# Queries of the first two units by seven products, and half of two weight sums moved to VectorE

## The chip, the cores and the metric

The kernel runs on one core of one Trainium2 chip. The core has five engines with a queue of instructions each: TensorE (PE in the profile; its weight loads are PEld), VectorE (DVE), ScalarE (ACT), GpSimd (POOL) and SyncE (SP, which here only issues DMAs). Each engine takes its instructions in order, and waits between engines are semaphores. The metric is the device time of one execution in microseconds (us), the median of several runs. All arrays are float32.

## The reference

One transformer layer with the normalisation behind each half. Its input is `x` of 2 batches x 512 tokens x 512 channels. Cut to what matters:

```python
q = x @ Wq + bq                 # 32 heads of 128
k = x @ Wk + bk; v = x @ Wv + bv   # 8 groups of 128
q, k = rope(q), rope(k)         # x1*cos - x2*sin, x1*sin + x2*cos
scores = q @ k.T / sqrt(128), causal mask, softmax
ctx = probs @ v                 # 4 query heads share one group's k and v
x = layernorm(x + ctx @ Wo + bo)
y = x @ W_base.T + b_base       # then 4 chosen experts of rank 8
alpha = softmax(log(prior[active] + 1e-12) + (x @ router_W.T + router_b)[active])
y += sum over experts e of 2 * alpha_e * (x @ lora_A[e].T) @ lora_B[e].T
out = layernorm(x + y)
```

Everything has to be computed; `active` (which experts) is an input, so the experts' rows are gathered on the chip.

## The kernel before

**Units and slots.** The work is cut into 16 units: unit `u` is one group of four query heads (`R = 4`) in one batch, with 512 queries and 512 keys (`S`). A unit has 16 slots, one for every block of 32 queries x 4 heads (`QB`, `BLK`). The function `slot(T)` writes out what each engine does in slot `T`, in order: the query products of a later unit, key and value products, output products of an earlier unit, `score(T)`, then, each some slots behind, the maximum with the mask (`masked_max`, DVE), the exponentials (ACT), the reciprocals and transposes (DVE), the trip of the probabilities through DRAM (`blocks_out` in slot 4p+7 and `blocks_in` in slot 4p+9 for tile p) and `weigh(p, j)` from slot 4p+12 (probabilities times v). Slots run from `T_BEGIN = -8`; score 0 is in slot 0. Work that fits no regular place is hung onto a slot with `put(slot, f)` and runs at that slot's end. The order is written by hand (`manual_schedule`), so each engine's queue is exactly the order in which `slot` and the code ahead of it call; only the first lines (constants, loads) are ordered by the framework.

**Before slot 0.** Lines 1034 to 1061 are a preamble: four transposes of x tiles of batch 0 into `xT` (channels on partitions), keys of unit 0 (`k_mm`, `k_rope`), `expert_rows` (thirteen small integer operations on DVE that make the gathers' indices from `active`, then two gathers on POOL's queue), the queries of unit 0, four tiles of v, and the transposes of batch 1. Queries of unit 0 are plain: for each head four matmuls of 128x128x512 into one PSUM bank (`q_mm`, `proj_mm`, L355). Queries of unit 1 are plain too, one such matmul in each of the slots -8 to 7.

**Seven products.** From unit 2 on, two heads at a time (`k` is 0 or 1, the pair) are computed as a 2x2 block product with seven block products in place of eight (Strassen-Winograd): `q_products(u, k, step)`, steps 1, 2, 6, 5, 7, 4, 3, each two matmuls of 128x128x256 (`product`, L434). It needs sums of the weights, `w_sums` (four operations on POOL, L421 to L424, the last of which writes over a block of the weight tile itself), sums of x, `x_sums` (four operations of 128x512 per batch on DVE, L413), and leaves partial results in two half banks, `qx` and `qy`:

- step 1 writes qx; ACT copies it out (`q_copy` "p1"). Step 6 adds onto qx after that copy; copy "u2". Step 7 adds onto qx after that; copy "u3". Step 4 adds onto qx after that; copy "c21". So each of 6, 7, 4 and the next pair's step 1 waits for one copy.
- step 2 writes qy; DVE adds it to what "p1" left (`q_sum` "p1"). Step 5 begins qy anew after that sum; `q_sum` "u3" reads it after copy "u3"; step 3 adds onto qy after that; `q_sum` "u2" reads it, and the next pair's step 2 waits for that sum.

In slot T the step is given by (T+24) mod 8: 2, 6, 5, 7, none, 4, 3, and the next pair's 1. The fifth of eight slots has no query product.

**The rotation** (`rope_step`) is three DVE operations per head (L368, L371, L375), then an addition on POOL (L376) into `qT` or `kT`. Plain queries are read from PSUM by these; queries of the seven products have been copied to SBUF before and are read there.

**Moved pieces.** `prior_weights` (the logarithm of the prior on ACT, small DVE operations, one tiny matmul `pl`), `gather_experts` (six gathers on POOL's queue), `lora_weights` (transposes of the gathered rows on PE into the bank `wx`, copied out by DVE, L285, L286 and L292) and the addition of the output bias to the eight x tiles (POOL, L885) hang on slots by `put`. Tiles of v for batch 1 and the next groups also go through the bank `wx`, in slots -1, 1, 3, 5, 11, 13, 15, 17.

**Output weights.** `ctx @ Wo` also goes by seven products; it needs four sums of Wo's blocks per weight set, `wo_sums` (L627): t1 = b12 - b11, t2 = b22 - t1, b12 = b22 - b12 in place, t4 = b21 - t2. For weight sets of two units they are on DVE; for the last two that need them (sets 6 and 7, of one unit each, `single`) all four are on POOL in the slot ahead of the unit's first output product. The third slot of the eight uses t2 (`wx<-wt,cs`).

Of the kernel before, what the change touches and what calls it, by code (L numbers as in the profile page):

```python
# [12 lines left out]
ALU = mybir.AluOpType  # L13
# [5 lines left out]
R = H // G  # L19
D = 128  # L20
# [9 lines left out]
def postln_layer_kernel(  # L30
# [59 lines left out]
    def unit(u):  # L90
        return units[u]

    def set_of(u):
        return u // B if u < MIXED else MIXED // B + u - MIXED

    def set_units(n):
        return [u for u in range(NU) if set_of(u) == n]
# [86 lines left out]
    for r in range(QB):  # L184
        nc.gpsimd.tensor_copy(maskw[ts(r, BLK), S - BLK :], tri[ts(r, BLK), r, :])
    nc.gpsimd.memset(eps_sb, LN_EPS)
    for z in zt:
        nc.gpsimd.memset(z, 0.0)

    bqk = setup.tile([NBIAS, D], F32, name="bqk")  # L190
    nc.scalar.dma_start(out=bqk[:H, :], in_=bq.rearrange("(h d) -> h d", d=D))
# [104 lines left out]
    def prior_weights(step):  # L296

        if step == 0:
            pr_eps = setup.tile([EA, 1], F32, name="pr_eps")
            nc.vector.tensor_scalar(pr_eps, pr_act, PRIOR_EPS, None, ALU.add)  # L300
            pr["lp"] = setup.tile([EA, 1], F32, name="lp")
            nc.scalar.activation(pr["lp"], pr_eps, AF.Ln)
        elif step == 1:
            lpb = setup.tile([EA, 1], F32, name="lpb")
            nc.vector.tensor_tensor(lpb, pr["lp"], rb_act, ALU.add)
            ones = setup.tile([EA, P], F32, name="ones")
            nc.vector.memset(ones, 1.0)
            pr["rep"] = setup.tile([EA, P], F32, name="lp_rep")
            nc.vector.tensor_scalar(pr["rep"], ones, lpb, None, ALU.mult)
        else:  # L310
            pl = ps_wo.tile([P, EA], F32, tag="wx", name="pl")
            nc.tensor.matmul(pl, lhsT=pr["rep"], rhs=ident[:EA, :EA], start=True, stop=True)
            nc.vector.tensor_copy(lp_bc, pl)
# [37 lines left out]
    def proj_mm(key, pool, tag, wt, cols, b, c):  # L351
        if c == 0:
            psq[key] = pool.tile([P, S], F32, tag=tag, name="pp")
            in_psum.add(key)
        nc.tensor.matmul(  # L355
            psq[key], lhsT=wt[:, c, cols], rhs=xT[:, c, ts(b, S)], start=(c == 0), stop=(c == KC - 1))
# [31 lines left out]
    def k_rope(u, part):  # L388
        if part == 0:
            k_of(u)  # L390
        rope_step(("k", u), H + unit(u)[0], part, kT[u])

    def q_mm(u, r, c, pool, tag):

        g, b = unit(u)
        proj_mm(("q", u, r), pool, tag, wqk["q", set_of(u), r // 2], ts(r % 2, D), b, c)

# [5 lines left out]
    ws = {}  # L406
    halves = {}

    def x_sums(b, step):
        b11, b12, b21, b22 = (  # L410
            xT[:, CH * k : CH * (k + 1), b * S + a * TH : b * S + (a + 1) * TH] for k in range(2) for a in range(2))
        t1, t2, t3, t4 = (xs[:, b, k] for k in range(4))
        nc.vector.tensor_tensor(  # L413
            *((t1, b12, b11), (t2, b22, t1), (t3, b22, b12), (t4, b21, t2))[step], ALU.subtract)

    def w_block(n, k, head, c_half):
# [115 lines left out]
    def q_rope(u, r, part):  # L532
        if u not in qT:
            qT[u] = work.tile([P, UNIT, R, BLK], F32, tag="qT", name=f"qT_{u}")
        rope_step(("q", u, r), unit(u)[0] * R + r, part, qT[u][:, :, r, :])
# [325 lines left out]
    def put(slot, f):  # L861
        extra.setdefault(slot, []).append(f)
# [4 lines left out]
        for c in range(KC):  # L867
            v_mm(gg, t, c, pool, tag)

    put(T_BEGIN, gather_experts)  # L870
    for n, gg, t in [(2 * t - 1, 0, TPB + t) for t in range(TPB)] + [(2 * t + 11, 1, t) for t in range(TPB)]:
        put(n, lambda gg=gg, t=t: v_tile(gg, t, ps_wo, "wx"))
        put(n + 1, lambda gg=gg, t=t: v_out(gg, t))
    for n in range(TPB):
        put(n, lambda n=n: x_sums(0, n))
        put(n + 12, lambda n=n: x_sums(1, n))
    for k in range(3):
        put(-4 + k, lambda k=k: prior_weights(k))
        if k < 2:
            put(12 + 4 * k, lambda k=k: lora_weights(k))  # L880
    put(1, lambda: load_q(1, 1))
    put(6, lambda: load_wv(1))
    put(17, lambda: load_wo(1))
    for t in range(NT):
        put(2 + t, lambda t=t: nc.gpsimd.tensor_tensor(x_sb[:, t, :], x_sb[:, t, :], bo_bc, ALU.add))  # L885

    def q_from(u, k):

# [33 lines left out]
    def wo_from(u):  # L922
        return UNIT * u + LAG_WO
# [3 lines left out]
    for n in range(NSETS - 2):  # L927
        single = len(set_units(n)) == 1
        for k in range(4):
            put(wo_from(set_units(n)[0]) + (-1 if single else (0, 1, 1, 3)[k]),  # L930
                lambda n=n, k=k, engine=nc.gpsimd if single else nc.vector: wo_sums(n, k, engine))


    weigh_at = {}
# [13 lines left out]
    def slot(T):  # L948

        uq, step = divmod(T + 24, UNIT)  # L950
        kq, step = divmod(step, 8)
        now = B <= uq < NU
        if now and step != 7 and step != 4:
            q_products(uq, kq, {0: 2, 1: 6, 2: 5, 3: 7, 5: 4, 6: 3}[step])
        un, kn = (uq, 1) if kq == 0 else (uq + 1, 0)
        if B <= un < NU and step == 7:
            q_products(un, kn, 1)
        plain_q = T - T_BEGIN < UNIT and divmod(T - T_BEGIN, QB)
        if plain_q:
            r, c = plain_q  # L960
            q_mm(1, r, c, *q_banks[r])
        uk, l = divmod(T + UNIT, UNIT)
        if 0 < uk < PLAIN_K and l < KC:
            k_mm(uk, l)
        kv, o = kv_at(T)
        if kv and o in KV_STEPS:
            kv_products(*kv, KV_STEPS[o])
        kw, sw = divmod(T - LAG_WO, 8)
        products = 0 <= kw < LAST // 8
        if products:  # L970
            wo_products(kw, sw)
        plain = plain_at.get(T)
        if plain:
            p, step_o = plain
            wo_mm(p, 2 * step_o)
            wo_mm(p, 2 * step_o + 1)
        if 0 <= T < T_END:
            score(T)
        for part, j in weigh_at.get(T, ()):
            weigh(part, j)  # L980

        if now and step in (0, 2, 4, 6):
            q_copy(uq, kq, ("p1", "u2", "u3", "c21")[step // 2])
        if kv and KV_OUT.get(o) in KV_ON_ACT:
            kv_out(*kv, KV_OUT[o])
        for part, j in weigh_at.get(T - 1, ()):
            if j == parts[part][1]:
                context_out(part)

        if 0 <= T - 3 < T_END:  # L990
            normalise(T - 3)
        if 0 <= T - 1 < T_END:
            masked_max(T - 1)
            exponentials(T - 1)
        if products:
            wo_adds(kw, sw)
        if sw == 0 and 0 < kw <= LAST // 8:
            wo_adds(kw - 1, 8)
        if now and step in (1, 5, 7):
            q_sum(uq, kq, {1: "p1", 5: "u3", 7: "u2"}[step])  # L1000
        if kv and o in KV_OUT and KV_OUT[o] not in KV_ON_ACT:
            kv_out(*kv, KV_OUT[o])
        if 0 <= T - 2 < T_END:
            reciprocals(T - 2)
        if 0 <= T - 4 < T_END:
            blocks_transposed(T - 4)
            if (T - 4) % QB == QB - 1:
                blocks_out((T - 4) // QB)
        if T % QB == 1 and 0 <= T // QB - 2 < NP:
            blocks_in(T // QB - 2)  # L1010
        if 0 <= (T - LAG_WO + 1) // 8 < LAST // 8 and (T - LAG_WO + 1) % 8 == 0:
            ctx_sums((T - LAG_WO + 1) // 8)

        ur, sr = divmod(T + 24 - 7, UNIT)
        kr, sr = divmod(sr, 8)
        if B <= ur < NU and sr < 6:
            q_rope(ur, 2 * kr + (sr < 3), sr % 3)
        r, part = divmod(T - T_BEGIN - QB, QB)
        if 0 <= r < R and part < 3:
            q_rope(1, r, part)  # L1020
        k_slots = (4, 5, 6) if uk < PLAIN_K else (11, 13, 14) if uk < NU - 1 else (3, 5, 6)
        if 0 < uk < NU and l in k_slots:
            k_rope(uk, k_slots.index(l))
        if plain and step_o:
            wo_out(p)
        for f in extra.pop(T, ()):
            f()
# [1 line left out]
    ctx.enter_context(tc.manual_schedule())  # L1029

    spare = ((ps_wo, "wx"), (ps_wo, "wy"), (ps_ctx, "ctx"), (ps_sc, "sc"))
    q_banks = ((ps_q, "qx"), (ps_q, "qy"), (ps_q, "qx"), (ps_wo, "wy"))

    idle = ps_sc.tile([P, 2 * P], F32, tag="sc", name="idle")
    for _ in range(3):
# [5 lines left out]
    nc.vector.tensor_copy(bqkT, tb)  # L1041
    for c in range(KC):
        k_mm(0, c)
    for part in range(3):
        k_rope(0, part)
    expert_rows()

    for r in range(R):
        for c in range(KC):
            q_mm(0, r, c, *q_banks[r])  # L1050
        for part in range(3):
            q_rope(0, r, part)
        if r == 2:
            for t in range(TPB, NT):
                transpose_token_tile(xT[:, :, ts(t, P)], x_sb[:, t, :], *spare[t % 2 + 2], nc.scalar.copy)
        elif r:
            v_tile(0, r // 2, *spare[r // 2 * 2])
            v_out(0, r // 2)
    for t in range(2, TPB):
        v_tile(0, t, *spare[t % 2 * 2])  # L1060
        v_out(0, t)

    T_SETUP = 20
    for T in range(T_BEGIN, T_SETUP):
# [189 lines left out]
```

## Time and profile before

| what | value |
|---|---|
| median of 5 runs | 825.78 us (825.49 to 826.32) |
| the profiled execution's own time | 825.63 us |
| its span, first to last instruction | 823.6 us |
| granted TensorE clock | 0.998 |
| busy: PE / DVE / ACT / POOL | 814.0 / 598.1 / 378.6 / 327.7 us |
| first key matmul of unit 0 | 7.75 us |
| slot -8 begins on PE (first query matmul of unit 1) | 34.1 us |
| slot 0 begins on PE | 43.3 us |
| slot 8 begins on PE | 62.0 us |
| slot 13 begins on PE | 71.5 us |

The table's last rows are starts of instructions in the timeline, counted from the span's start. The profile is of one execution. In the timeline a row has start, length, engine, source line, operation, output<-inputs, shape, and in brackets how long the engine was idle ahead of it and what ended that; rows of DVE and POOL overlap those of PE. "x4" joins four instructions: a float32 matmul stands as two instructions. In the chain of work that ended last, a row has start, length and what ran.

### The profile page before, as it was taken

To read this page: it belongs to the slowest core of one execution; us is meant where nothing else is said; L and a number is where in the kernel's file an instruction comes from. 1 tells how busy PE (TensorE), PEld (TensorE's weight loads), DVE (VectorE), ACT (ScalarE), POOL (GpSimd) and SP (SyncE) were. 2 spreads that over 40 slices of the span, in tenths; PEclk is the share of its full clock that TensorE was granted. 3 is DMA by queue.
4 is the path that set the end of the run, shared out by engine and by line. 5 is a ranking of instruction groups with operands and counts; after the bars stand their busy time and mean duration, and the time that the engine had idled before them with its cause. 6 is when DMAs were issued, how large, how long until landed. Compare 5 with 4: busy or idle time off the path is not lost.

```text
span 823.6 us, 11178 instructions
## 1 busy us (share of the span) xinstructions
PE 814.0 (99%) x3381; PEld 596.6 (72%) x3381; DVE 598.1 (73%) x1964; ACT 378.6 (46%) x1058; POOL 327.7 (40%) x374
## 2 busy tenths in 40 slices
PE   8999999999999999999999999999999999999997
PEld 5567777777777778777777878777777777555565
DVE  5368877677879886787867786787867678974445
ACT  1236454453545454545535454445535454563253
POOL 6464343511534445322443245353445625410032
PEclk9999999999999999999999999999999999999999
DMA  9015627445455636364544536365544636574211
GB/s 306 21 52 150 202 73 197 121 122 159 125 170 139 182 90 209 87 160 146 149 146 115 179 90 205 91 185 173 136 134 120 194 83 204 142 255 142 76 38 64
DMA packets 84414, 115.99 MB, mean 141 GB/s; under 512 B 6525, under 2 KB 64237, under 8 KB 82306
## 3 DMA queue, kind: packets, MB, share of 16 engines
q1 hardware_dynamic: 83682, 114.98, 48.4%
q8 instruction: 27, 0.44, 0.2%
q0 software_dynamic: 448, 0.14, 0.1%
q14 instruction: 33, 0.27, 0.1%
q10 hardware_dynamic: 224, 0.16, 0.1%
HBM read 71.21 MB, written 44.04 MB: 140 GB/s over the span
## 4 chain that ended last, share of the span: by engine, by line
PE 93%; DVE 3%; POOL 2%; ACT 1%; DMA 1%; issue 0%; SPq 0%; DVEq 0%; POOLq 0%
PE pc L602 16%; PE sc L546 14%; PE qx L434 11%; PE wx L434 11%; PE qy L434 9%; PE wy L434 8%; PE pp L355 5%; PE kx L434 4%; PE vx L512 4%; PE py L767 3%; PE po L674 3%; PE pv L338 3%; PE tp L275 1%; PE py L808 1%; DMA x_sb<-_attn_hidden_states_dram 1%
## 5 line engine op out<-in xcount | busy, mean ns | idle before, releaser
L554 DVE CUSTOM_DVE_ANT_0 sc<-sc,maskw 128x288 f32<-128x288 f32 (+15 forms) x256 | 114.2, 446 | 146.3 <-PE sc L546 144.7
L561 ACT ACTIVATE p<-sc,nmax 128x288 f32<-128x288 f32 (+15 forms) x256 | 124.1, 485 | 203.4 <-DVE nmax L554 180.6
L602 PE MATMUL pc<-pT,v 128*128 128x512 f32 x320 | 165.3, 599 | 0.0
L546 PE MATMUL sc<-kT,qT 128*128 128x160 f32 (+15 forms) x512 | 161.9, 398 | 0.2 <-ACT p L561 0.2
L376 POOL TENSOR_TENSOR qT<-q,t 128x512 f32<-128x512 f32 x56 | 76.4, 1364 | 171.4 <-DVE q L375 171.4
L569 ACT ACTIVATE p<-p,den 128x288 f32<-128x288 f32 (+15 forms) x256 | 133.2, 521 | 0.0
L546 PEld LDWEIGHTS sc<-kT,qT 128*128 128x128 f32 x512 | 95.9, 190 | 23.5 <-issue 9.6
L609 ACT ACTIVATE ctxT<-pc,bqkT 128x512 f32<-128x512 f32 x64 | 44.0, 687 | 117.6 <-PE pc L602 117.6
L421 POOL TENSOR_TENSOR cs<-ctxT 128x256 f32<-128x256 f32 x28 | 22.2, 793 | 157.8 <-PE wy L434 93.7
L577 DVE STREAM_TRANSPOSE zt<-p 128x128 f32<-128x128 f32 (+2 forms) x192 | 81.6, 425 | 0.0
L602 PEld LDWEIGHTS pc<-pT,v 128*128 128x128 f32 x320 | 57.1, 190 | 18.7 <-issue 5.7
L470 ACT COPY q<-qx 128x256 f32<-128x256 f32 x112 | 41.3, 369 | 36.5 <-PE qx L434 36.5
L434 PE MATMUL qx<-xs,wq 128*128 128x256 f32 x224 | 58.0, 381 | 0.0
L434 PE MATMUL wx<-wo,ctxT 128*128 128x256 f32 x224 | 57.6, 379 | 0.0
L434 PEld LDWEIGHTS qx<-xs,wq 128*128 128x128 f32 x224 | 41.4, 190 | 22.3 <-issue 18.4
L579 DVE STREAM_TRANSPOSE zt<-p 128x32 f32<-128x32 f32 (+3 forms) x256 | 57.4, 224 | 0.0
L561 ACT ACTIVATION_READ_ACCUMULATOR p<-sc,nmax 128x1 f32 x256 | 49.8, 195 | 0.0
L434 PEld LDWEIGHTS wx<-wo,ctxT 128*128 128x128 f32 x224 | 42.5, 190 | 7.7 <-issue 1.2
L368 DVE SCALAR_TENSOR_TENSOR t<-q,bqkT,rope_sb 64x512 f32<-64x512 f32 x56 | 46.0, 821 | 1.5
L660 DVE TENSOR_TENSOR x_sb<-wx,x_sb 128x256 f32<-128x256 f32 x112 | 47.0, 420 | 0.0
L371 DVE SCALAR_TENSOR_TENSOR t<-q,bqkT,rope_sb 64x512 f32<-64x512 f32 x56 | 43.4, 775 | 1.3
L565 DVE RECIPROCAL den<-den 128x1 f32<-128x1 f32 x256 | 39.2, 153 | 1.4 <-ACT p L561 1.2
(224 smaller groups left out, 1480.4 us busy)
## 6 DMA issues: line engine op xcount, KB each, us to landing
db<-zt SPq DMA_DIRECT2D x64, 256.0 KB, 4.1
pT<-db SPq DMA_DIRECT2D x16, 1024.0 KB, 4.8
db<-zt SPq DMA_DIRECT2D x64, 192.0 KB, 3.2
pT<-db SPq DMA_DIRECT2D x16, 768.0 KB, 4.3
wq<-in_L_attn_Wq_dram SPq DMA_DIRECT2D x20, 512.0 KB, 5.4
wo<-in_L_attn_Wo_dram SPq DMA_DIRECT2D x10, 1024.0 KB
db<-zt SPq DMA_DIRECT2D x64, 128.0 KB, 2.4
pT<-db SPq DMA_DIRECT2D x16, 512.0 KB, 4.0
```

The lines of the kernel that those rows point to most:

```text
L368: nc.vector.scalar_tensor_tensor(t2[lo, :], q[hi, :], b_ap[hi, :], rope_sb[hi, 1, :], ALU.add, ALU.mult)
L376: nc.gpsimd.tensor_tensor(dst, t1[:, :].rearrange("p (n s) -> p n s", s=BLK), t2[:, :].rearrange("p (n s) -> p n s", s=BLK), ALU.add)
L434: nc.tensor.matmul(ps, lhsT=wt[:, c, :], rhs=xt[:, c, :], start=start and c == 0, stop=c == CH - 1, skip_group_check=True)
L546: nc.tensor.matmul(sc[s][:, :w], lhsT=qT[u][:, i * QB + n].rearrange("p r s -> p (r s)"), rhs=kT[u][:].rearrange("p n s -> p (n s)")[:, :w ...
L554: nc.vector.tensor_tensor_reduce(sc[s][:, :w], sc[s][:, :w], maskw[:, S - w :], -SCALE, -MASKED, ALU.add, ALU.min, nmax[s])
L561: nc.scalar.activation(ptile[s][:, :w], sc[s][:, :w], AF.Exp, bias=nmax[s], scale=-1.0, accum_out=rden[s])
L569: nc.scalar.activation(ptile[s][:, :w], ptile[s][:, :w], AF.Copy, scale=rden[s])
L577: nc.vector.transpose(z[:, :, last - i : last, n, :].rearrange("p q j s -> p j q s"), ptile[s][:, : i * P])
L579: nc.vector.transpose(z[:, : n + 1, last, n, :], ptile[s][:, i * P : w])
L602: nc.tensor.matmul(psc[p], lhsT=v_sb[g // VG, b][:, j, ts(g % VG, D)], rhs=pT[p][:, :, ts(j, P)], start=(j == 0), stop=(j == i))
L609: nc.scalar.activation(ctxT[p], psc[p], AF.Identity, bias=bqkT[:, col : col + 1])
L660: nc.vector.tensor_tensor(into, pw[k, bank], into, ALU.add)
```

## The change

- Queries of units 0 and 1 go by the seven products. `q_mm` is gone. Unit 0's products stand in the preamble, with four tiles of v between them (`v_first`) and the transposes of batch 1 behind the first pair; unit 1's run in slots -8 to 7 by the same rule as those of later units.
- `x_sums` of batch 0 (four DVE operations) move from slots 0 to 3 into the preamble ahead of `expert_rows`; those of batch 1 from slots 12 to 15 into the second pair, two on DVE and two on POOL.
- `w_sums` of set 0 (twice four POOL operations) are new; the two memsets of `zt` move on POOL's queue from ahead of the issue of the small loads of `active` to behind the second `w_sums`.
- The rotation of k for unit 0 moves behind step 2 of the second pair; that of unit 0's third head (`q_rope(0, 2)`) into slots -8 to -6.
- The logarithm (`prior_weights(0)`) moves into the second pair; its later parts stay in slots -4 and -2. `gather_experts` goes from slot -8 to -5, `lora_weights` from slots 12 and 16 to 8 and 10, the output bias from slots 2 to 9 to slots 12 to 19.
- Of `wo_sums` of sets 6 and 7, t1 (still a slot ahead) and t2 (now in the first slot) go to VectorE; b12 and t4 stay on POOL, in the first slot.

```diff
@@ constants @@
-    for z in zt:
-        nc.gpsimd.memset(z, 0.0)
@@
-    def q_mm(u, r, c, pool, tag):
-        g, b = unit(u)
-        proj_mm(("q", u, r), pool, tag, wqk["q", set_of(u), r // 2], ts(r % 2, D), b, c)
@@
-    def x_sums(b, step):
+    def x_sums(b, step, engine=nc.vector):
...
-        nc.vector.tensor_tensor(
+        engine.tensor_tensor(
@@
-    put(T_BEGIN, gather_experts)
+    put(T_BEGIN + 3, gather_experts)
...
-    for n in range(TPB):
-        put(n, lambda n=n: x_sums(0, n))
-        put(n + 12, lambda n=n: x_sums(1, n))
-    for k in range(3):
-        put(-4 + k, lambda k=k: prior_weights(k))
-        if k < 2:
-            put(12 + 4 * k, lambda k=k: lora_weights(k))
+    for k in range(2):
+        put(-4 + 2 * k, lambda k=k: prior_weights(k + 1))
+        put(8 + 2 * k, lambda k=k: lora_weights(k))
...
-        put(2 + t, lambda t=t: nc.gpsimd.tensor_tensor(x_sb[:, t, :], x_sb[:, t, :], bo_bc, ALU.add))
+        put(12 + t, lambda t=t: nc.gpsimd.tensor_tensor(x_sb[:, t, :], x_sb[:, t, :], bo_bc, ALU.add))
@@
-            put(wo_from(set_units(n)[0]) + (-1 if single else (0, 1, 1, 3)[k]),
-                lambda n=n, k=k, engine=nc.gpsimd if single else nc.vector: wo_sums(n, k, engine))
+            put(wo_from(set_units(n)[0]) + ((-1, 0, 0, 0) if single else (0, 1, 1, 3))[k],
+                lambda n=n, k=k, engine=nc.gpsimd if single and k > 1 else nc.vector: wo_sums(n, k, engine))
@@ slot(T) @@
-        now = B <= uq < NU
+        now = 0 < uq < NU
...
-        if B <= un < NU and step == 7:
+        if un < NU and step == 7:
             q_products(un, kn, 1)
-        plain_q = T - T_BEGIN < UNIT and divmod(T - T_BEGIN, QB)
-        if plain_q:
-            r, c = plain_q
-            q_mm(1, r, c, *q_banks[r])
...
-        if B <= ur < NU and sr < 6:
+        if 0 < ur < NU and sr < 6:
             q_rope(ur, 2 * kr + (sr < 3), sr % 3)
-        r, part = divmod(T - T_BEGIN - QB, QB)
-        if 0 <= r < R and part < 3:
-            q_rope(1, r, part)
@@ the preamble @@
-    for part in range(3):
-        k_rope(0, part)
+    for n in range(4):
+        x_sums(0, n)
+    w_sums(0, 0)
     expert_rows()
-    for r in range(R):
-        for c in range(KC):
-            q_mm(0, r, c, *q_banks[r])
-        for part in range(3):
-            q_rope(0, r, part)
-        if r == 2:
-            for t in range(TPB, NT):
-                transpose_token_tile(xT[:, :, ts(t, P)], x_sb[:, t, :], *spare[t % 2 + 2], nc.scalar.copy)
-        elif r:
-            v_tile(0, r // 2, *spare[r // 2 * 2])
-            v_out(0, r // 2)
-    for t in range(2, TPB):
-        v_tile(0, t, *spare[t % 2 * 2])
-        v_out(0, t)
+    w_sums(0, 1)
+    for z in zt:
+        nc.gpsimd.memset(z, 0.0)
+
+    def v_first(t):
+        v_tile(0, t, *spare[t % 2])
+        v_out(0, t)
+
+    for k in range(2):
+        for step in (1, 2, 6, 5, 7):
+            q_products(0, k, step)
+            if step == 1:
+                q_copy(0, k, "p1")
+            elif step == 2:
+                q_sum(0, k, "p1")
+                if k:
+                    for part in range(3):
+                        k_rope(0, part)
+            elif step == 6:
+                q_copy(0, k, "u2")
+            elif step == 7:
+                q_copy(0, k, "u3")
+        q_sum(0, k, "u3")
+        if k:
+            for n in range(4):
+                x_sums(1, n, nc.gpsimd if n > 1 else nc.vector)
+        v_first(2 * k)
+        q_products(0, k, 4)
+        q_copy(0, k, "c21")
+        if k:
+            prior_weights(0)
+            for part in range(2):
+                q_rope(0, 3, part)
+        q_products(0, k, 3)
+        q_sum(0, k, "u2")
+        v_first(2 * k + 1)
+        if k == 0:
+            for t in range(TPB, NT):
+                transpose_token_tile(xT[:, :, ts(t, P)], x_sb[:, t, :], *spare[t % 2 + 2], nc.scalar.copy)
+        for part in range(2 * k, 3):
+            q_rope(0, 2 * k + 1, part)
+        for part in range(3):
+            if k:
+                put(T_BEGIN + part, lambda part=part: q_rope(0, 2, part))
+            else:
+                q_rope(0, 0, part)
+    q_products(1, 0, 1)
```

More of the change, by code (lines that the diff above doesn't have):

```diff
@@ L1031, in postln_layer_kernel @@
     spare = ((ps_wo, "wx"), (ps_wo, "wy"), (ps_ctx, "ctx"), (ps_sc, "sc"))
-    q_banks = ((ps_q, "qx"), (ps_q, "qy"), (ps_q, "qx"), (ps_wo, "wy"))
     idle = ps_sc.tile([P, 2 * P], F32, tag="sc", name="idle")
```

## Prediction

> **What bounds the kernel.** I read the busy times first, then the chain of work that ended last, what PE waited for, and then the timeline of the stretches that the change touches. PE comes first:
>
> ```profile
> PE 814.0 (99%) x3381; PEld 596.6 (72%) x3381; DVE 598.1 (73%) x1964; ACT 378.6 (46%) x1058; POOL 327.7 (40%) x374
> PEclk9999999999999999999999999999999999999999
> PE 93%; DVE 3%; POOL 2%; ACT 1%; DMA 1%; issue 0%; SPq 0%; DVEq 0%; POOLq 0%
> ```
>
> PE is busy 99% of the span at a full granted clock, and the chain lies on it for 93%. PE's waits of any size:
>
> ```profile
> PE wx L434 <- POOL wt L627: 1.3, 1, 1.3
> PE pp L355 <- ACT xT L276: 0.5, 1, 0.5
> PE sc L546 <- ACT p L561: 0.2, 1, 0.2
> ```
>
> So matmul time taken away is time won, unless a new wait takes its place; and one wait of 1.3 us is there to be removed. The other engines have room on average only. Prices for PE come from the chain:
>
> ```profile
> 20.04 3.43 PE pp L355 x8
> 34.30 6.01 PE pp L355 x14
> 62.15 0.86 PE qy L434 x4
> ```
>
> Eight instructions are four plain query matmuls: 0.857 us each. One product (four instructions) is 0.86; its spacing in the timeline (61.98 to 62.85) gives 0.87.
>
> **Part 1, the products.** Units 0 and 1 lose 2 x 16 plain matmuls (32 x 0.857 = 27.4) and gain 4 pairs x 7 products (28 x 0.867 = 24.3): 3.1 us less on PE, all of it ahead of slot 8. Key matmuls, v tiles and transposes stay. Also new are copies on ACT (16 x 0.37; ACT is busy 46%) and sums on DVE (12 x 0.42). ACT's copies cost where nothing stands between two products on one bank; DVE's cost where DVE is late.
>
> **What makes DVE late.** A DVE operation with two SBUF inputs and a POOL addition do not run side by side here; one waits for the other's end:
>
> ```profile
> 14.20 0.94 DVE L234 CUSTOM_DVE_ANT_0 full_er<-act_er,lift_er 32x2 uint16<-32x2 uint16 x1
> 13.85 1.28 POOL L376 TENSOR_TENSOR kT<-t,t 128x512 f32<-128x512 f32 x1 [4.46 <-DVE lift_e L232]
> 51.32 1.73 DVE L413 TENSOR_TENSOR xs<-xT,xs 128x512 f32<-128x512 f32 x1
> 50.01 4.16 POOL L885 TENSOR_TENSOR x_sb<-x_sb,bo_bc 128x512 f32<-128x512 f32 x3
> ```
>
> A 0.15 us integer operation lasts 0.94 and ends with POOL's addition at 15.13; a sum of x takes 1.73 beside the bias additions. By shape:
>
> ```profile
> L368 DVE SCALAR_TENSOR_TENSOR t<-q,bqkT,rope_sb 64x512 f32<-64x512 f32 x56 | 46.0, 821 | 1.5
> L368 DVE SCALAR_TENSOR_TENSOR t<-pp,bqkT,rope_sb 64x512 f32<-64x512 f32 x12 | 9.0, 755 | 17.8 <-PE pp L355 11.2 <-issue 6.3
> L371 DVE SCALAR_TENSOR_TENSOR t<-kT,bqkT,rope_sb 64x512 f32<-64x512 f32 x12 | 14.2, 1183 | 0.2
> L413 DVE TENSOR_TENSOR xs<-xT,xs 128x512 f32<-128x512 f32 x4 | 3.8, 940 | 0.1
> ```
>
> The rotation of plain queries reads PSUM (pp) and is spared; after the change eight more heads are rotated from SBUF. Averages rise little (755 to 821 ns); crowded places pay in full (1183, 940). I walked each new queue in order by these durations, once with full alternation and once without.
>
> *The Trainium skill, page "SBUF — State Buffer", section "Who interferes with whom", says that a DVE instruction with two SBUF inputs excludes a GpSimd instruction that reads SBUF, the later one waiting for the whole of the other. The rows above agree and show no exception; it speaks against this change, which puts eight heads' rotations under it. Taken for every meeting of the two engines it makes the time 825.1 (the first rival); by the mean rows, in which most operations meet nothing, it is 824.0.*
>
> **Part 2, the preamble's order.** PE runs 1, 2, 6, 5, 7, v, 4, 3, v, four transposes, then the second pair likewise, then unit 1.
> - A: step 5 of the first pair waits for `q_sum` "p1", queued on DVE behind four sums of x and eleven integer operations of `expert_rows`, which need the loads of `active`. Before, these landed at 11.7 to 14.0; their issue no longer stands behind two memsets (1.37 and 1.81), so about 3.2 earlier. Walked: 0.15; none if nothing blocks, 1.1 at full blocking. I take 0.1, as the loads should land before their turn. `k_rope` and the heads' rotations come later but their readers are in slot 0 and after.
> - B: step 2 of unit 1's first pair waits for `q_sum` "u2" of (0, 1), behind two sums of x, an epsilon addition and two thirds of `q_rope(0, 3)`, alternating with POOL's key addition (1.3) and its two sums of x (1.3 each). Walked with full blocking 0.8, at most 1.4, at least 0; taken 0.5, between.
> - C: slot -4 has no product and, unlike in later units, no scores: step 4 waits for copy "u3": 0.2 to start, 0.37 to run, 0.07 back, 0.65. This follows from the order alone.
> - Copies and starts elsewhere: each has a product or a v tile ahead of it; 0.1. The wait for xT (0.5) may go: not counted. Gathers moved three slots: their six issues on POOL's queue (some 1.27 each) now stand behind the heads' additions and ahead of `w_sums(1, 0)`, wanted several slots later; 0. The logarithm's table load (1.28 in the trace) on ACT stands behind copy "c21" of the second pair, and the next ACT work that PE needs, copy "p1" of unit 1, is a product and a v tile away; 0, counted in B's upper end.
>
> **Part 3, slots 0 to 19.** `x_sums` (8 x 0.75) leave slots 0 to 3 and 12 to 15 and the bias additions leave slots 2 to 9, which spares DVE there. But `lora_weights` now falls into slots 8 and 10:
> - D: DVE had 1.47 idle ahead of slot 8. Now in slots 7 to 11 come sums and rotations of unit 2, two copies of A and b (0.53), the copy of bmT (1.06), all beside POOL's key addition and `w_sums(1, 1)`.
>
> ```profile
> 62.19 0.43 DVE L554 CUSTOM_DVE_ANT_0 sc<-sc,maskw 128x256 f32<-128x256 f32 x1 [1.47 <-PE sc L546]
> 83.49 1.06 DVE L292 COPY bmT<-tbm 32x512 f32<-32x512 f32 x1 [1.56 <-PE tbm L291]
> ```
>
> Step 5 in slot 10 waits for `q_sum` "p1" (0.4 to 1.0) and the v tile of slot 11 waits until the copy of bmT has left the bank wx (0.3 to 0.8): together 0.3 to 2.0, taken 0.9, below the middle, as the mean rows show partial blocking. Before, in slots 12 and 16, DVE had idle time for them (1.56 ahead of that copy). PE's transposes for it are moved, not added. The bias additions in slots 12 to 19 meet the rotations of slots 15 to 20; the first tile of probabilities had 1.9 to spare at its first use (landed at 68.29, used at 70.17) and moves with its slots. 0, up to 0.5 in D's end.
>
> **Part 4, Wo's sums.** Set 6 had no wait and gets none (t2 ends two slots ahead of its use). Set 7 before:
>
> ```profile
> 692.76 1.23 POOL qT L376
> 693.98 1.69 POOL wt L627
> 695.74 1.27 POOL wt L627
> 697.06 1.13 PE wx L434 x4
> ```
>
> POOL reaches t2 only after the sums of ctx, and PE waits 1.31. With t1 and t2 on DVE (0.70 free, 1.125 blocked) I get t2 at 694.9 against a use at 695.75: the wait goes. What is late next is DVE's maximum (a score then waits for its bank), up to 2.7 behind where it had about 1 idle. Net 0.6 to 0.8 by the walk, -0.4 if the maximum is held in full, 1.3 if not at all; taken 0.8.
>
> **Sum.** 3.1 - (0.1 + 0.5 + 0.65 + 0.1 + 0.9) + 0.8 = 1.65, and I give 0.1 of the vanished xT wait back: 1.75. The profiled execution took 825.63 (span 823.6 and 2.0 around it), 0.15 under the median 825.78. So 823.9 on its scale, 824.0 as a median. 0.2% (1.65 us) is about what a measurement of this kernel can tell from no change: faster is below 824.1, slower above 827.4.
>
> **The rivals.**
> 1. Full alternation of DVE and POOL eats the saving. A 0.15, B 0.8, D 1.4, C 0.65, 0.1: 3.1 of 3.1 is gone and Wo's 0.7 stays: 825.1, no change. The crowded rows (1183, 1125) speak for it, the mean of 821 against.
> 2. Slower, by the same lock at its worst: DVE is so late in slots 7 to 11 and behind `expert_rows` that A, B and D cost 1.1, 1.4 and 2.0; with 0.75 that is 5.25, and at set 7 the maximum pays 0.4: 825.78 + 5.25 - 3.1 + 0.4 = 828.3. It decides from A + B + D = 3.1 - 0.75 + 1.65 = 4.0 (Wo at nothing), nearly every operation at its blocked price. Against it: DVE has idle time within those slots; for it: eight more heads in SBUF.
> 3. Wo's edit does nothing net (DVE's maximum gives the 1.3 back) while the rest is as forecast: 3.1 - 2.25 + 0.1 = 0.95: 824.8, no change.
>
> **How the numbers follow.** Forecast 0.48 (its own range 822.3 to 824.9, nearly all faster), rival 1 0.20, rival 2 0.23, rival 3 0.09. Low end: no blocking, 3.1 - 0.75 - D 0.3 + Wo 1.3 = 3.35: 822.4. High end 828.0, just short of rival 2's own number. Faster 0.45, same 0.31, slower 0.24.
>
> **What would show it.** Slot 0's first matmul at 43.2 (before 43.34) with PE waits at the four named places: step 5 for a DVE `q` (A), step 2 of unit 1 for `q` (B), step 4 in slot -4 for ACT `q` at 0.65 (C), step 5 and a v tile near slots 10 and 11 (D); slot 13 less than 0.5 from 71.5; no wait of `wx` for `wt` near 695, and the remainder between these unchanged. Wrong would make it: a wait for a DMA or for POOL's `w_sums(0, ...)` in the preamble, a lower granted clock, or a rotation late for a score in slot 0.

## The result and the profile after

The changed kernel takes 827.05 us (median of 31 runs, 826.48 to 829.96); the kernel before took 825.9 in the runs beside it (52 runs). The ratio is 1.0016, with a 95% interval of 1.0011 to 1.0021: slower, by 1.15 us, where 1.75 faster was forecast. It lies within the forecast's range, but on the other side of the kernel before. By the prediction's own lines (faster below 824.1, slower above 827.4) it counts as the same; the interval of the ratio, though, lies wholly above 1.

The profiled execution of the changed kernel took 826.67 us (span 824.9, granted clock 0.999), 1.04 more than that of the kernel before. Line numbers have moved: products are L427 (L434 before), the sums `q_sum` L467 (L474), the rotation L366, L369 and L373 (L368, L371, L375), its addition on GpSimd L374 (L376), sums of x L406 (L413), Wo's sums L620 (L627), maximum L547 (L554). First the busy times and the chain that ended last, from the page of the changed kernel:

```profile
PE 813.0 (99%) x3429; PEld 605.0 (73%) x3429; DVE 610.9 (74%) x1978; ACT 384.9 (47%) x1074; POOL 334.1 (40%) x380
PE 90%; DVE 6%; DMA 2%; issue 1%; POOL 1%; ACT 0%; SPq 0%; DVEq 0%; POOLq 0%; ACTq 0%
```

The chain has lost 3% of the span on PE (93% before) and gained 3% on DVE. What PE waited for:

```profile
PE qy L427 <- DVE q L467: 1.6, 2, 1.0
...
PE wx L427 <- DVE den L558: 0.6, 1, 0.6
PE qx L427 <- ACT q L463: 0.5, 1, 0.5
PE pp L353 <- ACT xT L274: 0.5, 1, 0.5
PE pv L336 <- DVE bmT L290: 0.3, 1, 0.3
```

Before there were 1.3 for Wo's sum and 0.5 for xT. The first is gone, the second is still there, and four new ones have come. Three stand at places that the prediction named: sums (qy, twice), the copy u3 (qx in slot -4) and the copy of bmT (pv). The fourth is behind DVE's late maximum at Wo's set 7, as it said, but at the bank of Wo's products (wx) and not at a score. These figures leave out the short idle times; the starts of PE's instructions give the whole of each wait. PE in the timeline of the changed kernel:

```profile
33.13 1.03 PE L427 MATMUL qx<-xT,wq 128*128 128x256 f32 x4
35.12 1.13 PE L427 MATMUL qy<-xT,wq 128*128 128x256 f32 x4 [0.97 <-DVE q L467]
...
37.99 1.03 PE L427 MATMUL qx<-xs,wq 128*128 128x256 f32 x4
39.53 1.13 PE L427 MATMUL qx<-xs,wq 128*128 128x256 f32 x4 [0.52 <-ACT q L463]
40.77 1.13 PE L427 MATMUL qy<-xT,ws 128*128 128x256 f32 x4
```

A product fills 0.867, so step 2 of unit 1 could have started at 34.00 and started 1.12 late (B). Step 4 in slot -4 was 0.67 late (C). Step 3, 40.77, was 0.37 late as well: a wait that the prediction didn't have. Near slots 10 and 11 step 5 was 0.83 late and the v tile 0.46 (D). The account by stretches, from such starts in both timelines:

| stretch on PE | after minus before at its end | saved by products | lost |
|---|---|---|---|
| to the first key matmul (8.06, 7.75) | +0.31 | 0 | 0.31, a later landing of x in this execution |
| to slot 0 (44.84, 43.34) | +1.50 | 1.50 (24 plain, now 22 products) | A 0.16, the same sum in the second pair 0.17, B 1.12, C 0.67, step 3 0.37, rest 0.2 |
| to slot 8 (61.80, 61.98) | -0.18 | 1.65 (8 plain and a product, now 7 products) | 0 |
| to slot 13 (73.28, 71.49) | +1.79 | 0 | D 0.83 + 0.46; 0.43 for transposes moved here from slot 16; rest 0.25 |
| to Wo's set 7 (691.91, 690.58) | +1.33 | 0.43 comes back | 0 |
| past it (702.65, 701.53) | +1.12 | 0.2 by Wo's sums | 0 |

The 0.31 of the first row is not shown to come from the change: in the fourteen profiles of this document the first key matmul starts at 7.75 to 8.60, and at 7.75, 7.87 and 8.42 in the three whose preamble is that of the kernel before.

So the products saved what was worked out (1.50 and 1.65 are by the prices; 1.68 was measured in slots 0 to 7), and the waits took 3.8 back. Why DVE was late at B is in its own timeline and in GpSimd's. First DVE, then POOL, of the changed kernel:

```profile
30.32 1.64 DVE L406 TENSOR_TENSOR xs<-xT,xs 128x512 f32<-128x512 f32 x1
31.88 0.13 DVE L298 TENSOR_SCALAR pr_eps<-pr_act 4x1 f32<-4x1 f32 x1
32.05 1.80 DVE L366 SCALAR_TENSOR_TENSOR t<-q,bqkT,rope_sb 64x512 f32<-64x512 f32 x1
33.87 0.74 DVE L369 SCALAR_TENSOR_TENSOR t<-q,bqkT,rope_sb 64x512 f32<-64x512 f32 x1
34.64 0.42 DVE L467 TENSOR_TENSOR q<-qy,q 128x256 f32<-128x256 f32 x1
```

```profile
29.69 1.72 POOL L406 TENSOR_TENSOR xs<-xT 128x512 f32<-128x512 f32 x1
32.04 1.27 POOL L406 TENSOR_TENSOR xs<-xT,xs 128x512 f32<-128x512 f32 x1 [0.63 <-DVE pr_eps L298]
```

The sum that PE waited for (34.64) stands behind a sum of x at 1.64 (0.69 free) and a rotation step at 1.80 (0.75 free), each of which began while GpSimd added. The same timeline shows what does not block: during `zt`'s memsets on GpSimd, 18.39 to 21.51, two rotation steps that read SBUF took 0.75 and 0.74; and a step that reads PSUM (t<-pp) took 0.76 beside an addition. This is the section "Who interferes with whom" of the Trainium skill's page "SBUF — State Buffer", row for row: two SBUF inputs, and a GpSimd instruction that reads.

### The profile page after: what moved, and what is told of

It reads as the page before. It is cut to its first block, busy times and chain, and to the rows that moved or that the text cites. A ratio compares the mean times of both kernels' runs of the same rounds, so it can differ in the third digit from the quotient of the medians.

```text
span 824.9 us, 11321 instructions
## 1 busy us (share of the span) xinstructions
PE 813.0 (99%) x3429; PEld 605.0 (73%) x3429; DVE 610.9 (74%) x1978; ACT 384.9 (47%) x1074; POOL 334.1 (40%) x380
## 4 chain that ended last, share of the span: by engine, by line
PE 90%; DVE 6%; DMA 2%; issue 1%; POOL 1%; ACT 0%; SPq 0%; DVEq 0%; POOLq 0%; ACTq 0%
PE pc L595 16%; PE sc L539 13%; PE qx L427 12%; PE wx L427 11%; PE qy L427 9%; PE wy L427 8%; PE kx L427 4%; PE vx L505 4%; PE py L760 3%; PE po L667 3%; PE pv L336 2%; PE pp L353 2%; PE tp L273 1%; PE py L801 1%; DVE t L369 1%
## 5 line engine op out<-in xcount | busy, mean ns | idle before, releaser
L547 DVE CUSTOM_DVE_ANT_0 sc<-sc,maskw 128x288 f32<-128x288 f32 (+15 forms) x256 | 114.2, 446 | 147.4 <-PE sc L539 145.7
L554 ACT ACTIVATE p<-sc,nmax 128x288 f32<-128x288 f32 (+15 forms) x256 | 124.1, 485 | 202.3 <-DVE nmax L547 181.2
L374 POOL TENSOR_TENSOR qT<-q,t 128x512 f32<-128x512 f32 x64 | 87.5, 1367 | 181.1 <-DVE q L373 181.1
L463 ACT COPY q<-qx 128x256 f32<-128x256 f32 x128 | 47.3, 369 | 57.5 <-PE qx L427 55.9
L427 PE MATMUL qx<-xs,wq 128*128 128x256 f32 x256 | 66.2, 381 | 0.5 <-ACT q L463 0.5
L427 PEld LDWEIGHTS qx<-xs,wq 128*128 128x128 f32 x256 | 47.3, 190 | 24.1 <-issue 18.9
L427 PE MATMUL wx<-wo,ctxT 128*128 128x256 f32 x224 | 57.7, 380 | 0.6 <-DVE den L558 0.6
L366 DVE SCALAR_TENSOR_TENSOR t<-q,bqkT,rope_sb 64x512 f32<-64x512 f32 x64 | 55.1, 861 | 1.8
L369 DVE SCALAR_TENSOR_TENSOR t<-q,bqkT,rope_sb 64x512 f32<-64x512 f32 x64 | 50.4, 787 | 1.5
L554 ACT ACTIVATION_READ_ACCUMULATOR p<-sc,nmax 128x1 f32 x256 | 49.9, 195 | 0.0
L427 PEld LDWEIGHTS wx<-wo,ctxT 128*128 128x128 f32 x224 | 42.4, 190 | 8.6 <-issue 2.1
L373 DVE SCALAR_TENSOR_TENSOR q<-q,bqkT,rope_sb 128x512 f32<-128x512 f32 x64 | 46.1, 721 | 0.1
```

The source lines that it names most:

```text
L366: nc.vector.scalar_tensor_tensor(t2[lo, :], q[hi, :], b_ap[hi, :], rope_sb[hi, 1, :], ALU.add, ALU.mult)
L369: nc.vector.scalar_tensor_tensor(t2[hi, :], q[lo, :], b_ap[lo, :], rope_sb[lo, 1, :], ALU.add, ALU.mult)
L374: nc.gpsimd.tensor_tensor(dst, t1[:, :].rearrange("p (n s) -> p n s", s=BLK), t2[:, :].rearrange("p (n s) -> p n s", s=BLK), ALU.add)
L427: nc.tensor.matmul(ps, lhsT=wt[:, c, :], rhs=xt[:, c, :], start=start and c == 0, stop=c == CH - 1, skip_group_check=True)
L463: nc.scalar.copy(q_half(u, k, name), halves[u, k]["qx"])
L547: nc.vector.tensor_tensor_reduce(sc[s][:, :w], sc[s][:, :w], maskw[:, S - w :], -SCALE, -MASKED, ALU.add, ALU.min, nmax[s])
```

## Experiments

My theory after these traces: PE's gain is real; it is given back in separate waits, each made by what stands ahead of one DVE or ACT operation in its queue, and most of it by DVE and GpSimd excluding each other. The main rivals: DVE simply has too much to do, in whatever order (a wait removed at one place comes back at the next), and DVE is late by its own queue, without GpSimd. Each kernel's time is a median of 7 to 12 executions, beside 25 or more of the kernel before, whose medians were 825.9, 825.96 and 825.83 in the three groups. The changed kernel's 827.05 is the one above.

**1. Wo's sums.** The first run is the kernel before with this one edit; the second is the changed kernel without it.

> The kernel before with the edit of Wo's sums alone. My theory now: PE gained 3.1 us from the products and lost it to waits for DVE; Wo's edit removed a wait of 1.31 but DVE then came late at the next bank, so that PE's lead between 690 and 702 changed by about 0.2 to 0.3 only. Expected 0.2 to 0.3 under the kernel before (825.6), no wait of wx for wt, and a wait of about 0.6 of wx for DVE two slots later. If the forecast's 0.8 was right: 825.1. If all is given back: 825.9.

> The changed kernel with Wo's sums as before. By the same theory 0.2 to 0.3 above the changed kernel: 827.3; by the forecast's 0.8: 827.9. If the edit lost time, as a rival has it: below 827.0.

Measured 825.55 (ratio to before 0.9994, interval 0.9985 to 1.0003) and 827.19 (1.0015, 1.0006 to 1.0024). The edit is worth 0.35 in one kernel and 0.14 in the other, not 0.8; neither difference is clear of zero by itself, but in both most of the wait of 1.31 has only changed its place. The longest of PE's waits behind its start, in the first run:

```profile
PE wx L434 <- DVE den L565: 0.7, 1, 0.7
```

wx no longer waits for wt but for DVE, which empties the bank behind a late maximum. DVE ahead of that wait, in the timeline of the changed kernel:

```profile
699.15 1.61 DVE L366 SCALAR_TENSOR_TENSOR t<-q,bqkT,rope_sb 64x512 f32<-64x512 f32 x1
700.79 0.43 DVE L547 CUSTOM_DVE_ANT_0 sc<-sc,maskw 128x256 f32<-128x256 f32 x1
...
701.14 0.42 DVE L653 TENSOR_TENSOR x_sb<-wx,x_sb 128x256 f32<-128x256 f32 x1
```

The same maximum in the kernel before:

```profile
698.66 0.43 DVE L554 CUSTOM_DVE_ANT_0 sc<-sc,maskw 128x256 f32<-128x256 f32 x1 [1.11 <-PE sc L546]
```

There DVE was idle for 1.11 ahead of it. In the changed kernel it begins at 700.79, behind the rotation step, and the addition that frees the bank ends at 701.56; the product starts at 701.71.

**2. The rotation behind the sum (B).**

```diff
-            for part in range(2):
-                q_rope(0, 3, part)
         q_products(0, k, 3)
         q_sum(0, k, "u2")
+        if k:
+            for part in range(2):
+                q_rope(0, 3, part)
```

> The changed kernel with two thirds of the rotation of unit 0's fourth head put behind the last sum of (0, 1) on DVE. My theory (each wait is a matter of what stands ahead in DVE's queue): the wait of step 2 of unit 1 (1.13 late) goes, 825.9 to 826.1. Rival, DVE has too little time in this stretch whatever the order: the wait comes back at step 5 or at step 3, and the time stays at 826.7 or more.

Measured 826.2 (1.0003, 0.9994 to 1.0012): 0.85 less, within 0.1 of the theory's number. But PE's rows, in the timeline of this kernel, speak for the rival's mechanism:

```profile
34.93 1.03 PE L427 MATMUL qx<-xT,wq 128*128 128x256 f32 x4
35.79 1.03 PE L427 MATMUL qy<-xT,wq 128*128 128x256 f32 x4
36.66 1.03 PE L427 MATMUL qx<-xs,ws 128*128 128x256 f32 x4
38.49 1.13 PE L427 MATMUL qy<-xs,ws 128*128 128x256 f32 x4 [0.81 <-DVE q L467]
```

Step 2 now follows at once, but step 5, two products later, is 0.97 late, where it was 0.06 late in the changed kernel: the rotation is only ahead of another sum. Starts can't be compared between the two timelines: in this profiled execution, and in that of experiment 3, the granted clock was 0.5 to 0.65 between 8 and 12 us, and the eight key matmuls took 5.4 in place of 3.7. Distances can. From step 1 of unit 1's first pair to step 1 of its second it is 8.69 (34.93 to 43.62), in the changed kernel 9.02 (33.13 to 42.15). So 0.33 is won in this stretch, and where the rest of the 0.85 comes from is not shown. Order alone moves this wait by two products, and 0.97 of 1.12 remains.

**3. All sums of x on VectorE.** This gives DVE more to do and GpSimd less: `x_sums(1, n)` in place of `x_sums(1, n, nc.gpsimd if n > 1 else nc.vector)`.

> The changed kernel with all four sums of x of batch 1 on VectorE, none on GpSimd: DVE gets two operations more (2 x 0.7), GpSimd two fewer. If DVE and GpSimd exclude each other, DVE was waiting for those two anyway (one sum of x at 1.64, the rotation's first step at 1.80): DVE reaches the sum that step 2 of unit 1 waits for at most 0.3 later, and the time is 827.0 plus or minus 0.3. If they run side by side and DVE is late only by its own queue, that sum comes 1.4 later: 828.4.

Measured 826.14 (1.0005, 0.9996 to 1.0014): 0.9 less, more than either theory had. DVE in its timeline:

```profile
31.01 1.33 DVE L406 TENSOR_TENSOR xs<-xT 128x512 f32<-128x512 f32 x1
32.38 0.69 DVE L406 TENSOR_TENSOR xs<-xT,xs 128x512 f32<-128x512 f32 x1
...
34.35 0.75 DVE L366 SCALAR_TENSOR_TENSOR t<-q,bqkT,rope_sb 64x512 f32<-64x512 f32 x1
35.12 0.74 DVE L369 SCALAR_TENSOR_TENSOR t<-q,bqkT,rope_sb 64x512 f32<-64x512 f32 x1
35.90 0.42 DVE L467 TENSOR_TENSOR q<-qy,q 128x256 f32<-128x256 f32 x1
```

From the first sum of x to the `q_sum` it takes 4.9 (31.01 to 35.90), where the changed kernel took 5.7 (28.95 to 34.64) with two operations fewer. The other two sums of x take 0.69 as well. What is left of the exclusion there is in the first row, 1.33 beside GpSimd's addition for the keys. On PE step 2 of unit 1 (36.38, step 1 at 35.19) is 0.32 late in place of 1.12, and the distance of experiment 2 is 8.22 in place of 9.02. A queue that only does its own work can't get shorter by two more operations: this decides for the exclusion.

**4. Work for PE in slot -4 (C).** The v tile of slot -1 goes to slot -4 (`n = -4 if n == -1 else n`).

> The changed kernel with the v tile of slot -1 moved into slot -4, where no product stands, so that PE has 1.73 of work while copy u3 runs. My theory: the waits of step 4 for that copy (0.67) and of step 3 for sum u3 (0.38) go: 826.0 to 826.4. Rival, DVE is the bound of this stretch and the time is only waited out later (at step 2 of slot 0 for sum u2): 827.0.

Measured 825.93 (0.9998, 0.9989 to 1.0007): 1.12 less, for 0.67 and 0.37 worked out. The rival falls: nothing of it is waited out later in that stretch; the next products stand without a gap from 39.02 to 42.5. Its profiled execution has another wait, 1.3 for a tile of probabilities on its trip through DRAM; run 8 asks whether that is the next limit.

**5. The logarithm's DVE operations behind sum u3.** `put(-4 + 2 * k` becomes `put(-3 + 2 * k`.

> The changed kernel with the two later parts of the prior's logarithm one slot later each, so that the three small operations on DVE (one of them 1.18 beside a GpSimd addition) stand behind sum u3, not ahead of it. My theory: the wait of step 3 for that sum (0.38) goes: 826.7. Rival, the queue of DVE moves the same 0.4 to the next slot: 827.05.

Measured 826.76 (1.0013, 1.0003 to 1.0022): 0.3 less, nearer to the theory's number; the difference is small beside the spread of either kernel. PE's rows of this execution don't show it. Step 3's wait is gone (40.85, behind step 4 at 39.89), but the tiny matmul `pl`, a slot later too, now waits for ACT's copy of the v tile:

```profile
44.93 0.38 PE L310 MATMUL pl<-ident,lp_rep 4*128 4x4 f32 x2 [0.46 <-ACT v L345]
```

From step 4 to the first product of slot 0 it is 5.35 (39.89 to 45.24), in the changed kernel 5.31 (39.53 to 44.84). So in this execution the 0.4 is waited out in the next slot, as the rival has it, though on ACT and not in DVE's queue. The cause of step 3's wait in the changed kernel's DVE timeline:

```profile
39.20 1.18 DVE L307 TENSOR_SCALAR lp_rep<-ones,lpb 4x128 f32<-4x128 f32 x1
40.31 0.40 DVE L467 TENSOR_TENSOR q<-qy,q 128x256 f32<-128x256 f32 x1
```

The 4x128 operation takes 0.34 in the kernel before and 0.28 in this experiment; beside GpSimd's addition it takes 1.18.

**6. The gathered rows back in slots 12 and 16 (D).** `put(8 + 2 * k` becomes `put(12 + 4 * k`.

> The changed kernel with the gathered rows' transposes and copies back in slots 12 and 16. My theory: the two waits near slots 10 and 11 (0.84 and 0.45 late) go: 825.7 to 825.9. Rival, DVE is short of time in slots 7 to 11 through the seven products' own sums and rotations: step 5 still waits, 826.6 or more.

Measured 827.62 (1.0027, 1.0015 to 1.0038): 0.57 more, against the theory and within the rival's "826.6 or more". Step 5 still waits 0.71 of idle time, so the copies of A and b were not its cause. The v tile's wait is gone, but a new one of 1.03 stands at 103.08: a step 2 waits for a sum u2 on DVE. The sum it waits for stands behind Wo's first sum, which meets an addition of GpSimd. GpSimd and DVE of this kernel (first fence) and of the changed one (second):

```profile
96.47 1.26 POOL L374 TENSOR_TENSOR qT<-q,t 128x512 f32<-128x512 f32 x1
96.91 1.38 DVE L620 TENSOR_TENSOR wt<-wo 128x512 f32<-128x512 f32 x1
```

```profile
95.01 1.26 POOL L374 TENSOR_TENSOR qT<-q,t 128x512 f32<-128x512 f32 x1
96.94 0.69 DVE L620 TENSOR_TENSOR wt<-wo 128x512 f32<-128x512 f32 x1
```

DVE begins the sum at the same time in both; it is GpSimd that is 1.46 late. It has been so since its addition to q at 87.35 (85.89 in the changed kernel), which waits for the last step of a rotation, and that step stands on DVE behind the copy of bmT (84.42, 1.07 long). The bias additions and the sums of ctx carry the delay on. Wo's third sum takes 1.75 here and 1.76 in the changed kernel, and so makes no difference. That it is the copy that does it, and not the transposes, is read from the rows and wasn't tried alone.

**7. Sums of the weights away from slots 7 to 10 (D).** `w_sums(1, 1)` goes to slot 11 in place of 6.

> The changed kernel with the second sums of the weights of set 1 (four GpSimd operations) in slot 11 in place of slot 6, so that GpSimd adds nothing beside the rotation of unit 1's last head in slots 7 to 10. If the two engines exclude each other, the rotation's steps fall from 1.12 and 0.97 to 0.75, the sum ahead of step 5 comes 0.6 earlier, and step 5's wait (0.84 late) shrinks to 0.2 or less: 826.4. If DVE is late only by the gathered rows' copies and its own queue: the steps stay as they are and the time at 827.05.

Measured 826.42 (1.0009, 1.0000 to 1.0019): 0.63 less, as the exclusion has it. DVE of this kernel (first fence) and of the changed one (second), the two steps of the rotation of unit 1's last head and the sum ahead of step 5:

```profile
61.77 0.75 DVE L366 SCALAR_TENSOR_TENSOR t<-q,bqkT,rope_sb 64x512 f32<-64x512 f32 x1
...
63.38 0.74 DVE L369 SCALAR_TENSOR_TENSOR t<-q,bqkT,rope_sb 64x512 f32<-64x512 f32 x1
...
64.89 0.42 DVE L467 TENSOR_TENSOR q<-qy,q 128x256 f32<-128x256 f32 x1
```

```profile
61.75 1.12 DVE L366 SCALAR_TENSOR_TENSOR t<-q,bqkT,rope_sb 64x512 f32<-64x512 f32 x1
...
63.72 0.97 DVE L369 SCALAR_TENSOR_TENSOR t<-q,bqkT,rope_sb 64x512 f32<-64x512 f32 x1
...
65.45 0.42 DVE L467 TENSOR_TENSOR q<-qy,q 128x256 f32<-128x256 f32 x1
```

Same operations, same place in the queue, 0.75 and 0.74 in place of 1.12 and 0.97; the sum is 0.56 earlier and step 5, at 65.36, is 0.24 late in place of 0.83. In the kernel before the same head's rotation read PSUM and took 0.76 and 0.74 beside these very additions of GpSimd.

**8. The three best together.** The edits of 3, 4 and 7.

> The changed kernel with three edits that were run alone together: all sums of x of batch 1 on VectorE (0.9 faster alone), the v tile in slot -4 (1.1), the second sums of the weights of set 1 in slot 11 (0.6). My theory, separate waits, each at its own place: the gains add, 824.4. Rival, PE ahead only meets the next late thing (the trip of the first probabilities through DRAM, 1.3 in the profile of the v-tile kernel): 825.2 to 825.6.

Measured 824.59 (0.9989, 0.9979 to 0.9999). The three alone sum to 0.91 + 1.12 + 0.63 = 2.66; together 2.46, and no wait for probabilities is listed in this execution. In PE's rows the gains stand at the three places: 0.8 at step 2 of unit 1, 1.2 from slot -4 to slot 0 and 0.6 at step 5 of slot 10. The waits are separate, and the kernel is now faster than the kernel before, by 1.24, with an interval that lies just below 1.

**9. Wo's sums without DVE.** On top of 8, and also in the kernel before by itself:

```diff
-            put(wo_from(set_units(n)[0]) + ((-1, 0, 0, 0) if single else (0, 1, 1, 3))[k],
-                lambda n=n, k=k, engine=nc.gpsimd if single and k > 1 else nc.vector: wo_sums(n, k, engine))
+            put(wo_from(set_units(n)[0]) + ((-2, -2, 0, 0) if single else (0, 1, 1, 3))[k],
+                lambda n=n, k=k, engine=nc.gpsimd if single else nc.vector: wo_sums(n, k, engine))
```

> The same with all four of Wo's sums of sets 6 and 7 on GpSimd, but the first two ahead of the sums of ctx, where GpSimd was idle for 5.9: the wait for t2 goes without work for DVE. My theory, the edit won only 0.3 of 1.3 because DVE came late: 0.7 to 1.0 under the kernel with the three edits. Rival, DVE was late there anyway, by GpSimd's additions: no difference.

> The kernel before with the first two of Wo's sums of sets 6 and 7 on GpSimd ahead of the sums of ctx, and nothing else. My theory: the wait of 1.31 goes and nothing on DVE is late: 824.7 to 825.0. If DVE's lateness comes with PE's lead and not with the two operations: 825.6, as with the edit alone.

Measured 823.5 (0.9973, 0.9962 to 0.9984), 1.09 under the three edits, a little more than the theory had; and 824.78 (0.9989, 0.9980 to 0.9998) for the kernel before with this alone, 1.05 under it, where the move to DVE had won 0.35. GpSimd in the latter's timeline:

```profile
687.53 1.45 POOL L627 TENSOR_TENSOR wt<-wo 128x512 f32<-128x512 f32 x1 [3.81 <-PE wx L434]
689.06 1.60 POOL L627 TENSOR_TENSOR wt<-wo,wt 128x512 f32<-128x512 f32 x1
690.62 1.17 POOL L421 TENSOR_TENSOR cs<-ctxT 128x256 f32<-128x256 f32 x1
```

t2 is ready at 690.66, 5.6 ahead of its use at 696.27, mostly in time that GpSimd had spent idle (5.88 in the kernel before, until 688.92), and wx's wait for DVE is 0.2. So 1.05 of the 1.31 could be had; the change took it from GpSimd's queue and put most of it into DVE's.

**10. The gathered rows one slot earlier.** On top of 9, `put(7 + 2 * k` in place of `put(8 + 2 * k`.

> The same again with the gathered rows' transposes and copies in slots 7 and 9 in place of 8 and 10, so that a whole slot stands between the copy of bmT and the v tile that needs its bank. My theory: the wait of that v tile (0.45 late) goes: 0.3 to 0.5 under the last. Rival, DVE carries the copy's 1.06 into the next sum: no difference.

Measured 823.17 (0.9972, 0.9964 to 0.9981), 0.33 less as a difference of medians, though the two intervals overlap. The wait of the v tile for bmT is gone from PE's list; in its place stand, in this execution, the wait for a tile of probabilities that experiment 4 also had, and one for ACT's exponentials:

```profile
PE pc L595 <- DMA pT<-db: 0.8, 1, 0.8
PE sc L539 <- ACT p L554: 0.6, 2, 0.4
```

What makes that trip late in some executions and not in others (0.7 in the second run of experiment 1, none in run 8) stays open. This version beats both kernels, by 2.7 and 3.9 us.

## Why the prediction was wrong

What failed is the price put on the waits for DVE. The sum took 2.25 for A, B, C, D and the copies, and 3.78 was measured; and Wo's 0.8 came to 0.14 to 0.35. With that a saving of 3.1, which was right, became a loss.

- **What bounds the kernel, part 1 (3.1 less on PE)**: right. The starts give 1.68 in slots 0 to 7, worked out 1.65.
- **"What makes DVE late"**: the mechanism was right, its size was the error. I let "crowded places pay in full" stand beside a mean of 821 against 755 and took middle values. The mean is over the first steps of 56 rotations in 14 units; 45 of them took 0.77 or less and the other 11 from 0.99 to 1.25. The preamble and slots 7 to 11 are crowded places, and there GpSimd's operation was waited out to its end: 1.80, 1.67, 1.64 and 1.12 for operations of 0.69 to 0.75. The walk with full alternation (the first rival) comes nearest, with waits of 3.1; but it lacked the late sum below and kept 0.7 for Wo's sums, so its 825.1 is still 2 too low.
- **A**, 0.1: measured 0.16; right. The same sum in the second pair cost 0.17 more, which "copies and starts elsewhere; 0.1" was to hold.
- **B**, 0.5 (at most 1.4): measured 1.12. This is the largest mis-sized term of the preamble. Experiment 3 shows its cause: with the two sums of x off GpSimd, 0.32 is left. Experiment 2 shows that order alone leaves 0.97.
- **C**, 0.65: measured 0.67; right, and experiment 4 gets it back.
- **"Copies and starts elsewhere ... 0.1"**: wrong. It was worked out for ACT's copies; step 3 also needs `q_sum` "u3", and ahead of that on DVE stand the logarithm's three small operations, one of them 1.18. I costed this move for ACT (the table load) and for PE, and not for DVE's queue: 0.37.
- **D**, 0.9: measured 0.83 + 0.46. The part at the v tile was the copy of bmT, as told; the part at step 5 was GpSimd's weight sums against the rotation (experiment 7) and remains with the copies gone (experiment 6). "Moved, not added" held for the transposes.
- **Part 4, Wo**, 0.8 (from -0.4 to 1.3): measured 0.35 and 0.14. The wait went, as said, and "what is late next is DVE's maximum" was right; it was later than the walk had it, since the rotation step ahead of it took 1.61.
- **"0.1 of the vanished xT wait"**: it didn't vanish (0.5 in both lists).

With the measured terms the sum is 3.1 - (0.33 + 1.12 + 0.67 + 0.37 + 1.29) + 0.2 = -0.5: slower. The medians differ by 0.65 more; the account shows 0.45 of that as "rest", single gaps of about 0.1 behind the waits, and what is left is within the spread of the runs. The second rival had the right sign and the wrong place and size: the waits after `expert_rows` stayed small, and A + B + D came to 2.7 with the second pair's sum, not 4.0; the sum that no term held (0.37) and Wo's missing 0.6 did the rest.

## What to carry to other kernels

Before giving an engine's saving a value, walk each new queue with every pair of DVE and GpSimd operations that can meet at the full price of one waiting for the other; a mean over the whole run says what the average place pays, and a change is made in one place. Moving an operand from PSUM to SBUF, or work to an idle GpSimd, can cost the other engine more than the work: giving VectorE two operations more and GpSimd two fewer made this kernel 0.9 us faster. A small operation is priced for the engine it runs on too: what stands behind it in that queue is what it costs.

## What the runs showed of the hardware

That the exclusion reaches a 4x128 operation with one array and one scalar per partition (lp_rep, 1.18 beside an addition of GpSimd, 0.28 and 0.34 otherwise) was not counted by the prediction. Memsets on GpSimd didn't hold up rotation steps that read SBUF (0.75 and 0.74 during them). And a wait costs PE somewhat more than the idle time listed. A product's row lasts 1.03 where the next one follows after 0.867, so idle time is counted from 0.16 later on: C is listed at 0.52 and delays the start by 0.67. The first product behind a wait is longer by 0.1 in its row (1.13), and the next one starts 0.1 later (0.97 behind it, as in 35.12 to 36.09).
